# More of layer 1 inside the last attention slot, the last block's first row finished by itself, and the last softmax sums on TensorE

## The chip, the cores and the metric

The kernel runs on one core of a Trainium2 chip. The metric is the time of one execution on the device in microseconds (us). The kernel before was run three times: 3644.64, 3645.58 and 3648.83 us, a median of 3645.58 us. One more execution was recorded by the profiler; it took 3646.8 us, and its first to last instruction span 3645.1 us. All times inside the kernel are from that execution, counted from its first instruction.

## The reference

The input is four images of 64 x 64 pixels with 256 channels, in float32. Two layers are applied in turn.

```python
# layer 0: full self-attention over the 4096 pixels of an image
q = x @ Wq + bq                     # 32 channels
k = x @ Wk + bk                     # 32 channels
v = x @ Wv + bv                     # 256 channels
attn = softmax(einsum('bnd,bmd->bnm', q, k))
x = gamma * einsum('bnm,bmc->bnc', attn, v) + x
# layer 1: perception, two pointwise layers, 3 x 3 local attention
perceived = depthwise_conv3x3(x, w_perc) + b_perc     # 3 outputs per channel: 768
hid = gelu(w_up1 @ perceived + b_up1)                 # 512
h = x + w_up2 @ hid + b_up2                           # 256
q, k, v = split(h @ w_qkv.T + b_qkv)
s[i] = (q * shifted(k, i)).sum(channels) / 16         # i: the 9 neighbours, zero padding
out = h + sum_i softmax(s)[i] * shifted(v, i)
```

The convolution needs the rows above and below a pixel, so a block of rows of layer 1 can be finished only when layer 0 has finished the first row of the next block. The local attention again reaches one row into the next block.

## The kernel before, in words

An image is cut into 8 blocks of 8 rows (512 pixels, `NB`), so there are 32 blocks, numbered 0 to 31 over the four images. The main loop (`for slot in range(NSLOT)`, L695) takes one block of layer 0 per slot. A slot has 16 points. At a point TensorE adds four products of weights and values to the two accumulators of the block (`product`, L279 to L291), at every second point it makes four banks of energies (`energy`, L262), ScalarE takes their exponential (`weight`, L274), and VectorE adds the weights up for the softmax denominator (`add_up`, L293). After the last point `finish` (L305) sums the denominator over the partitions with one product into `dps`, VectorE takes the reciprocal, and scales the two accumulators and adds them to the image held in SBUF (`xp`, seen as `xv`).

Layer 1 follows behind. While slot s runs, VectorE computes the convolution of block s-2 (`perceive`, L337: for each of six output groups one ScalarE operation for the first tap and eight VectorE operations L366, "taps", for the others), TensorE does the pointwise layers of block s-3 (`hidden` L380, four jobs of six products with a Gelu on ScalarE; `update` L405, two jobs into `dx`), then the local attention: `guide` L484 (the rotated queries `g`, copied to `lq`), `scores` L564 (`s`, exponentials `lp`, a mask), `local_values` L533 (`lv`), `border` L505 (`c`, the part of the denominator that comes from the zero padding), `local_sum` L601 (adds the weights up over the pieces into `lsum`), `local_denominator` L629 (one product `ld`, a reciprocal `lrden`) and `local_product` L636 (`lo`, the result). `jobs` (L701) says which of these stands at which point of a slot.

The order on each engine is the order in which the program calls these functions: the kernel is written out by hand, without a scheduler, and every engine takes its instructions in order. An instruction that uses another engine's result, or overwrites what another engine still reads, waits for it; these waits are put in when the program is built, from the tiles that the instructions touch.

PSUM has eight banks: two for the tag `m`, two for `acc`, and the four banks of the one tile `e`. During the slots every job of layer 1 takes a bank from `m`. After the last slot, in the tail, the list `turns` (L774) hands the jobs banks in the order `m, e, acc, m, acc`; a job that gets `e` allocates a new four-bank tile and uses only its first bank (`job_bank`, L98 to L103).

In the last slot (31) VectorE also does three of the six output groups of block 30's convolution, without the block's last row (`extra`, L720 to L724), since that row needs the first row of block 31. After `finish(31)` the tail (L774 to L812) does the rest: the missing rows and groups of block 30, all of the convolution of block 31, the pointwise layers of blocks 29, 30 and 31, and the local attention of blocks 27 to 31. For the last two blocks VectorE does the mask and the sum, for the others GpSimd.

All along, GpSimd adds intermediate results into one tile (`watch`, L158 to L160). At the very end VectorE tests that this tile stayed within bounds (L814 to L823); a register is loaded from the answer, and a slower path (`shifted`) would be taken if it had not.

Of the kernel before, what the change touches and what calls it, by code (L numbers as in the profile page):

```python
# [40 lines left out]
WATCH_MAX = 1.0e25  # L41
# [6 lines left out]
def attention_then_perception_kernel(  # L48
# [34 lines left out]
    def unshifted():  # L83
# [14 lines left out]
        def job_bank(name):  # L98
            turns.append(turns.pop(0))
            if turns[-1] == "e":  # L100
                return psum.tile([P, GRP, NB], F32, tag="e", name=name, bufs=1)[:, 0, :]
            return bank(turns[-1], name)
# [202 lines left out]
        def finish(s):  # L305
            g = s % NBLK
            den = sums.pop(s)

            dps = bank("m", f"dps_{s}")
            nc.tensor.matmul(dps, lhsT=ones, rhs=den[:, 0, :], start=True, stop=True)  # L310
            rden = tile_of([P, NB], "rden", f"rden_{s}", 2)
            nc.vector.reciprocal(rden, dps)  # L312
            os = []
            for c, acc in enumerate(accs.pop(s)):
                o = tile_of([P, NB], "o", f"o_{s}_{c}", 3)
                nc.vector.scalar_tensor_tensor(o, acc, gam[:, 0:1], rden, ALU.mult, ALU.mult)
                os.append(o)
            for c, o in enumerate(os):
                dst = xv[:, c, 1 + g * RB : 1 + (g + 1) * RB, 1 : 1 + W]
                nc.vector.tensor_tensor(  # L320
                    dst, o.rearrange("p (h w) -> p h w", w=W), dst, ALU.add
                )
            watch(den[:, 0, :])
            watch(rden)
            for o in os:
                watch(o)
# [10 lines left out]
        def perceive(s, parts):  # L337
# [5 lines left out]
            def first(i, r0, r1):  # L343
                if i not in percs[s]:
                    if not ahead:
                        perc = tile_of([P, NB], "perc", f"perc_{s}_{i}", NPERC)
                    else:

                        if i % 2 == 0:
                            percs[s, i] = spare(f"perc_{s}_{i}")  # L350
                        perc = percs[s, i - i % 2][:, i % 2, :]
                    percs[s][i] = perc
                tap_of(i, r0, r1, 0)

            def tap_of(i, r0, r1, tap):
# [12 lines left out]
            for n, part in enumerate(parts):  # L368
                if n == 0 or not ahead:
                    first(*part)  # L370
                if ahead and n + 1 < len(parts):
                    first(*parts[n + 1])
                for tap in range(1, TAPS):
                    tap_of(*part, tap)
                    if part[2] - part[1] > 1 or tap % 4 == 0:
                        yield

        whole = [(i, 0, RB) for i in range(NPC)]
# [105 lines left out]
        def guide(s, i):  # L484
# [7 lines left out]
            if s == NSLOT:  # L492
                return
# [11 lines left out]
        def border(s):  # L505
# [19 lines left out]
            pad = tile_of([1, 2 * RB + W], "pad", f"pad_{s}")  # L525
            nc.scalar.activation(pad[:, :n], ps[0:1, :n], AF.Exp, bias=bc, scale=-(C**-0.5))
            nc.gpsimd.tensor_scalar(pad[:, :n], pad[:, :n], 3.0, None, ALU.mult)
            pads[s] = pad

# [3 lines left out]
        def local_values(s, t):  # L533
# [8 lines left out]
            for half in range(2):  # L542
                if s < NSLOT:
                    lvs[s, t, half] = tile_of([P, C], "lv", f"lv_{s}_{t}_{half}", 8)
                else:
# [3 lines left out]
                nc.vector.tensor_tensor(  # L549
                    lvs[s, t, half], ps[:, half * C : (half + 1) * C], blv, ALU.add  # L550
                )
# [12 lines left out]
        def scores(s, half):  # L564
# [4 lines left out]
            tiles, rows = (2, QR) if s < NSLOT else (1, UP)  # L569
            n = tiles * rows * QW  # L570
            for t in range(tiles):
                for kin in range(CH):
# [5 lines left out]
                        rhs=guides[0][:, kin, t * KR : t * KR + rows, columns(half)],  # L578
# [17 lines left out]
            if g == 0:  # L596
                nc.gpsimd.memset(p[P // 2 :, : UP * QW], 0.0)
                if s < NSLOT:
                    nc.gpsimd.memset(p[: P // 2, UP * QW : QR * QW], 0.0)

        def local_sum(s):  # L601
# [12 lines left out]
            pad = pads.pop(s)  # L614
            side = pad[:, : 2 * RB].rearrange("p (w h) -> p h w", w=2)
            edge = one[:, :, 0 : W : W - 1]
            nc.gpsimd.tensor_tensor(edge, edge, side, ALU.add)
            for at, row in ((0, 0), (NBLK - 1, RB - 1)):
                if g == at:
                    above = pad[:, 2 * RB :]  # L620

                    ends = above[:, 0 : W : W - 1]
                    nc.gpsimd.tensor_scalar(ends, ends, 2.0 / 3.0, None, ALU.mult)
                    line = one[:, row, :]
                    nc.gpsimd.tensor_tensor(line, line, above, ALU.add)
# [3 lines left out]
        def local_denominator(s):  # L629
            ps = job_bank(f"ld_{s}")  # L630
            nc.tensor.matmul(ps, lhsT=ones, rhs=lsums.pop(s), start=True, stop=True)  # L631
# [4 lines left out]
        def local_product(s, c):  # L636
# [13 lines left out]
            watch(o)  # L650
# [44 lines left out]
        for slot in range(NSLOT):  # L695
# [24 lines left out]
            extra = iter(())  # L720
            if slot == NSLOT - 1:

                extra = perceive(slot - 1, [(i, 0, RB - 1) for i in range(NPC // 2)])
            for point in range(points):  # L724
# [22 lines left out]
                while stepped < min(n_steps, -(-(point + 1) * n_steps // (points - 2))):  # L747
                    next(conv, None)
                    stepped += 1
                    if stepped % 2:  # L750
                        next(extra, None)
# [17 lines left out]
            for _ in chain(conv, extra):  # L769
                pass  # L770
            finish(slot)


        turns[:] = ["m", "e", "acc", "m", "acc"]  # L774
        conv = chain(
            perceive(
                NSLOT - 2,
                [(i, RB - 1, RB) for i in range(NPC // 2)] + whole[NPC // 2 :],
            ),
            perceive(NSLOT - 1, whole),  # L780
        )
# [7 lines left out]
        last = NSLOT - 1  # L789
        for k in range(NSLOT - LAG_HID, NSLOT):  # L790
            a = k - LAG_ATT + LAG_HID
            if k == last:
                for _ in conv:
                    pass
            run(
                (hidden, k, 0, 6), (hidden, k, 1, 6), (local_denominator, a, 0),
                (hidden, k, 2, 6), (local_product, a, 0, 1), (hidden, k, 3, 6),
# [422 lines left out]
```

## Time and profile before

| | |
|---|---|
| median of three runs | 3645.58 us |
| span of the profiled execution | 3645.1 us |
| TensorE (PE) matmul busy | 3599.6 us, 99% of the span |
| VectorE (DVE) busy | 2448.6 us, 67% |
| ScalarE (ACT) busy | 1176.8 us, 32% |
| GpSimd (POOL) busy | 721.2 us, 20% |
| start of the last `dps` product, that is, the end of slot 31 | 3466.1 us |
| end of the last VectorE operation (L823) | 3638.0 us |

The engines are PE (TensorE matmul), PEld (its weight loads), DVE (VectorE), ACT (ScalarE), POOL (GpSimd) and SP (the queue that issues most transfers). In a line of the profile `L366` is the line of the kernel file, `perc<-xp,wperc,perc` are the tiles written and read, and after the `|` come the busy time, the mean duration of one instruction in ns, and the time that the engine had been idle just before such an instruction, with what ended the idleness. One float32 product of the program appears as two matmul records. A view of waits has lines `engine line waited for: us in total, times, longest us`. A wait for several things is put down to the one that came last.

### The profile page before, as it was taken

The numbers are of one execution on the slowest core, as the hardware profiler recorded it, in microseconds if no ns is written. First come the engines' busy times: TensorE is split into PE (matmuls) and PEld (weight loads), VectorE is DVE, ScalarE is ACT, GpSimd is POOL, SyncE is SP. The second block draws the span as 40 slices with busy tenths as digits, with TensorE's granted clock in tenths as the row PEclk, the third lists the DMA queues.
The fourth block names the chain that finished last, engine by engine and source line by source line (L and its number), as shares of the span: only waits on it lengthen the run. The fifth ranks groups of instructions, "written<-read, shape, count | busy, mean of one in ns | idle before, by whom it ended". The sixth has DMA issues, their size and how long they took to land.

```text
span 3645.1 us, 29412 instructions
## 1 busy us (share of the span) xinstructions
PE 3599.6 (99%) x11350; PEld 1706.7 (47%) x11350; DVE 2448.6 (67%) x2727; ACT 1176.8 (32%) x1324; POOL 721.2 (20%) x725
## 2 busy tenths in 40 slices
PE   9999999999999999999999999999999999999987
PEld 4444444454444444455444444444544444444444
DVE  3385676657666767766677667676666776766884
ACT  2233333323333333332333333333333333333321
POOL 1010112111222221121112222211121122222232
PEclk9999999999999999999999999999999999999999
DMA  3000000010000000101000000011100000000000
GB/s 103 6 3 4 0 9 21 18 44 15 15 15 3 12 15 15 27 23 38 15 15 15 15 3 12 15 27 33 28 15 15 15 15 15 4 12 15 6 10 21
DMA packets 84532, 64.68 MB, mean 18 GB/s; under 512 B 57280, under 2 KB 62528, under 8 KB 84256
## 3 DMA queue, kind: packets, MB, share of 16 engines
q1 hardware_dynamic: 83568, 62.19, 6.3%
q8 instruction: 91, 1.49, 0.2%
q10 hardware_dynamic: 816, 0.53, 0.0%
q14 instruction: 57, 0.47, 0.0%
HBM read 41.52 MB, written 18.81 MB: 17 GB/s over the span
## 4 chain that ended last, share of the span: by engine, by line
PE 97%; DVE 2%; issue 0%; ACT 0%; POOL 0%; DMA 0%; SPq 0%; ACTq 0%; DVEq 0%; POOLq 0%
PE acc L287 49%; PE hid L385 18%; PE e L268 7%; PE dx L411 6%; PE lv L537 3%; PE g L496 3%; PE v L234 3%; PE s L573 2%; PE lo L642 2%; DVE perc L366 1%; PE qk L200 1%; PE ld L631 1%; PE dps L310 1%; DVE lrden L633 0%; DVE rden L312 0%; PE c L520 0%
## 5 line engine op out<-in xcount | busy, mean ns | idle before, releaser
L287 PE MATMUL acc<-p,v 128*128 128x512 f32 x4096 | 1842.2, 595 | 0.1
L366 DVE SCALAR_TENSOR_TENSOR perc<-xp,wperc,perc 128x512 f32<-128x512 f32 (+2 forms) x1560 | 1305.9, 840 | 314.7 <-ACT perc L362 280.7
L287 PEld LDWEIGHTS acc<-p,v 128*128 128x128 f32 x4096 | 769.4, 190 | 917.3 <-issue 913.5
L276 ACT ACTIVATE p<-e 128x1024 f32<-128x1024 f32 x512 | 524.4, 1024 | 1516.1 <-PE e L268 904.1
L385 PE MATMUL hid<-perc,wup 128*128 128x512 f32 x1536 | 689.2, 598 | 1.6 <-DVE perc L366 1.6
L301 DVE TENSOR_TENSOR den<-den,p 128x1024 f32<-128x1024 f32 x480 | 597.0, 1244 | 44.3 <-ACT p L276 40.6
L385 PEld LDWEIGHTS hid<-perc,wup 128*128 128x128 f32 x1536 | 284.2, 190 | 391.4 <-issue 384.3
L268 PE MATMUL e<-qa,ka 32*128 32x512 f32 x2048 | 292.0, 640 | 0.0
L160 POOL TENSOR_TENSOR watched<-watched,lo 128x512 f32<-128x512 f32 x64 | 130.4, 2037 | 624.4 <-DVE lo L649 624.1
L411 PE MATMUL dx<-hid,wup 128*128 128x512 f32 x512 | 232.8, 598 | 0.0
L389 ACT ACTIVATE hid<-hid,bup 128x512 f32<-128x512 f32 x128 | 88.0, 687 | 400.3 <-PE hid L385 400.3
L312 DVE RECIPROCAL rden<-dps 128x512 f32<-128x512 f32 x32 | 107.4, 3358 | 160.4 <-PE dps L310 160.4
L592 POOL TENSOR_TENSOR lp<-lp,near 128x396 f32<-128x396 f32 x60 | 58.1, 970 | 739.0 <-ACT lp L588 739.0
L276 ACT ACT_TABLE_LOAD x116 | 148.8, 1283 | 151.2 <-issue 120.1
L549 DVE TENSOR_TENSOR lv<-lv,blv 128x256 f32<-128x256 f32 x130 | 49.2, 420 | 193.2 <-PE lv L537 193.2
L633 DVE RECIPROCAL lrden<-ld 128x512 f32<-128x512 f32 x32 | 107.4, 3357 | 82.3 <-PE ld L631 82.3
L417 DVE SCALAR_TENSOR_TENSOR h<-dx,bup,xp 128x256 f32<-128x256 f32 x128 | 56.0, 480 | 152.1 <-PE dx L411 149.3
L268 PEld LDWEIGHTS e<-qa,ka 32*128 32x128 f32 x2048 | 79.9, 182 | 164.6 <-issue 162.0
L411 PEld LDWEIGHTS dx<-hid,wup 128*128 128x128 f32 x512 | 94.7, 190 | 129.2 <-issue 120.2
L362 ACT ACTIVATE perc<-xp,bperc,wperc 128x512 f32<-128x512 f32 (+2 forms) x195 | 154.6, 796 | 0.0
L389 ACT ACT_TABLE_LOAD x119 | 152.7, 1283 | 2.2
L537 PE MATMUL lv<-wlv,h 128*128 128x256 f32 x520 | 128.6, 390 | 12.3 <-DVE h L417 11.0
(91 smaller groups left out, 2030.9 us busy)
## 6 DMA issues: line engine op xcount, KB each, us to landing
xp<-in_x SPq DMA_DIRECT2D x30, 528.0 KB, 4.1
out<-lo SPq DMA_DIRECT2D x60, 256.0 KB, 2.0
xc<-in_x SPq DMA_DIRECT2D x48, 256.0 KB, 3.8
qa<-packed SPq DMA_DIRECT2D x124, 64.0 KB, 2.1
ka<-st SPq DMA_DIRECT2D x124, 16.0 KB, 1.8
packed<-st SPq DMA_DIRECT2D x31, 64.0 KB, 1.9
wup<-in_w_up SPq DMA_DIRECT2D x1, 1536.0 KB, 7.0
xp<-in_x SPq DMA_DIRECT2D x4, 264.0 KB, 3.9
```

What stands on the lines that cost most here:

```text
L160: nc.gpsimd.tensor_tensor(watched, watched, values, ALU.add)
L234: nc.tensor.matmul(ps[:, i * C : (i + 1) * C], lhsT=xc[:, kin, bass.ts(2 * pair + i, P)], rhs=wv[:, kin, :], start=(kin == 0), stop=(kin = ...
L268: nc.tensor.matmul(e[:, j, :], lhsT=key[rows, :], rhs=queries[s][rows, :], start=True, stop=True,)
L276: nc.scalar.activation(p, energies[s, G][:, 2 * half : 2 * half + 2, :], AF.Exp)
L287: nc.tensor.matmul(accs[s][c], lhsT=v[:, 2 * half + i, bass.ts(c, P)], rhs=p[:, i, :], start=(first and i == 0), stop=(G == NG - 1 and hal ...
L301: nc.vector.tensor_tensor(den, den, p, ALU.add)
L362: nc.scalar.activation(acc, win, AF.Identity, bias=bperc[:, half, j : j + 1], scale=wt)
L366: nc.vector.scalar_tensor_tensor(acc, win, wt, acc, ALU.mult, ALU.add)
L385: nc.tensor.matmul(ps, lhsT=wup1[:, i, bass.ts(d, P)], rhs=percs[s][i], start=(i == 0), stop=(i == NPC - 1),)
L389: nc.scalar.activation(hids[s][:, d, :], ps, AF.Gelu, bias=bup1[:, d : d + 1])
L411: nc.tensor.matmul(ps, lhsT=wup2[:, d, bass.ts(c, P)], rhs=hids[s][:, d, :], start=(d == 0), stop=(d == NHC - 1),)
L537: nc.tensor.matmul(ps[:, half * C : (half + 1) * C], lhsT=keys_of(s, t, half, kin), rhs=wlv[:, kin, :], start=(kin == 0), stop=(kin == CH ...
```

## The change

There are six edits. Nothing before slot 31 is touched: on every engine the list of instructions is the same up to a point inside slot 31.

1. In slot 31 the list `jobs` is replaced. The jobs of block 28 stand closer together, and the points after them take in the four `hidden` jobs, both `update` jobs and both `local_values` jobs of block 29, with `local_sum`, `local_denominator` and `local_product` of block 27 and `border` of block 28. `guide` and `scores` of block 29 stay in the tail.
2. VectorE's list for slot 31 becomes the whole convolution of block 29 and then, for all six groups of block 30, the taps that need no row of block 31, and the others without the last row (`upper`). It was three groups of block 30, one step for every two of block 29.
3. `finish` becomes a generator, and for block 31 it works in two parts: row 0, and later rows 1 to 7. Between the two stand the 18 taps of block 30's last row (`lower`), and on TensorE the `guide` jobs of block 29.
4. In the tail `spread` is allocated once, as a four-bank tile, and the jobs are given slices of it in the order `spread[0], spread[1], m, spread[2], spread[3], m`.
5. The last block's `local_sum` is dropped. `local_denominator(31)` instead makes eight products of `ones` with the pieces of the weights, and with the border weights laid into a zeroed tile.
6. The watching changes: for the last blocks GpSimd adds the squares of the local values (twelve operations of 128 x 256) and the weights instead of the last sum and the last results; the test at the end sums the tile first (one reduction and two operations on 128 x 1), with the bound 1e22 for 1e25.

```diff
         def job_bank(name):
             turns.append(turns.pop(0))
-            if turns[-1] == "e":
-                return psum.tile([P, GRP, NB], F32, tag="e", name=name, bufs=1)[:, 0, :]
-            return bank(turns[-1], name)
+            return bank("m", name) if turns[-1] == "m" else turns[-1]
...
-        def finish(s):
+        def finish(s, parts=((0, RB),)):
...
+            for r0, r1 in parts:
+                n = slice(r0 * W, r1 * W)
+                nc.vector.reciprocal(rden[:, n], dps[:, n])
+                for c, o in enumerate(os):
+                    nc.vector.scalar_tensor_tensor(
+                        o[:, n], acc[c][:, n], gam[:, 0:1], rden[:, n], ALU.mult, ALU.mult
+                    )
...
+                if r1 == RB:
+                    watch(den[:, 0, :])
+                    watch(rden)
+                    for o in os:
+                        watch(o)
+                yield
...
+        LOW = TAPS - 3
+        upper = [
+            part for i in range(NPC)
+            for part in ((i, range(LOW), 0, RB), (i, range(LOW, TAPS), 0, RB - 1))
+        ]
+        lower = [(i, range(LOW, TAPS), RB - 1, RB) for i in range(NPC)]
...
+                if s >= NSLOT - 1:
+
+                    square = tile_of([P, 2, NB], "den", f"lv_{s}_{t}_{half}_2")[:, 0, :C]
+                    nc.gpsimd.tensor_tensor(square, lv, lv, ALU.mult)
+                    nc.gpsimd.tensor_tensor(watched[:, :C], watched[:, :C], square, ALU.add)
...
         def local_denominator(s):
             ps = job_bank(f"ld_{s}")
-            nc.tensor.matmul(ps, lhsT=ones, rhs=lsums.pop(s), start=True, stop=True)
+            if s < NSLOT - 1:
+                nc.tensor.matmul(ps, lhsT=ones, rhs=lsums.pop(s), start=True, stop=True)
+            else:
+
+                pv = ps.rearrange("p (h w) -> p h w", w=W)
+                side, line = both(pads["last"])
+                todo = [
+                    (pv[:, rows, columns(half)], near_ws[block, half][:, t, of, :])
+                    for half in range(2) for (block, t), rows, of in pieces(s)
+                ]
+                todo += [(pv[:, :, 0 : W : W - 1], side), (pv[:, RB - 1, :], line)]
+                for i, (to, p) in enumerate(todo):
+                    nc.tensor.matmul(
+                        to, lhsT=ones, rhs=p, start=(i == 0), stop=(i == len(todo) - 1),
+                        skip_group_check=True,
+                    )
...
-            extra = iter(())
             if slot == NSLOT - 1:
 
-                extra = perceive(slot - 1, [(i, 0, RB - 1) for i in range(NPC // 2)])
+
+                jobs = [
+                    job(hidden, k, 0), job(hidden, k, 1) + job(local_denominator, a),
+                    job(hidden, k, 2), job(local_product, a, 0) + job(hidden, k, 3),
+                    job(local_product, a, 1) + job(update, k, 0),
+                    job(update, k, 1) + job(local_values, k, 0),
+                    job(guide, k, 0) + job(local_values, k, 1), job(guide, k, 1),
+                    job(scores, k, 0) + job(hidden, k + 1, 0),
+                    job(scores, k, 1) + job(local_sum, k - 1) + job(hidden, k + 1, 1),
+                    job(hidden, k + 1, 2) + job(local_denominator, a + 1),
+                    job(hidden, k + 1, 3), job(update, k + 1, 0) + job(border, k),
+                    job(local_product, a + 1, 0) + job(update, k + 1, 1),
+                    job(local_product, a + 1, 1) + job(local_values, k + 1, 0),
+                    job(local_values, k + 1, 1),
+                ]
+                conv = chain(conv, perceive(slot - 1, upper))
+                n_steps += NPC * (TAPS - 1 + 3)
...
-        turns[:] = ["m", "e", "acc", "m", "acc"]
...
+        spread = psum.tile([P, GRP, NB], F32, tag="e", name="spread", bufs=1)
+        turns[:] = [spread[:, 0], spread[:, 1], "m", spread[:, 2], spread[:, 3], "m"]
+        last = NSLOT - 1
+        conv = perceive(last, whole)
...
+        finishing = finish(last, ((0, 1), (1, RB)))
+        next(finishing)
+        run((guide, last - 2, 0, 0), (guide, last - 2, 1, 0))
+        for _ in perceive(last - 1, lower):
+            pass
+        next(finishing)
         run(
...
+            (scores, last - 2, 0, 1), (scores, last - 2, 1, 1), (local_sum, last - 3, 0),
+            (hidden, last - 1, 0, 6), (hidden, last - 1, 1, 6), (local_denominator, last - 3, 0),
+            (hidden, last - 1, 2, 6), (local_product, last - 3, 0, 1), (hidden, last - 1, 3, 6),
+            (local_product, last - 3, 1, 1), (border, last - 2, 0), (update, last - 1, 0, 4),
+            (update, last - 1, 1, 4), (local_values, last - 1, 0, 2), (guide, last - 1, 0, 2),
+            (local_values, last - 1, 1, 2), (guide, last - 1, 1, 2), (scores, last - 1, 0, 2),
+            (scores, last - 1, 1, 2), (local_sum, last - 2, 0),
+        )
+        for _ in conv:
+            pass
...
-        test = [tile_of([P, NB], "o", f"test_{i}", 3) for i in range(2)]
...
+        good = tile_of([P, 3], "good", "good")
+        nc.vector.tensor_reduce(good[:, 0:1], watched, axis=AX.X, op=ALU.add)
```

A number after the function and its block in `run` is how many taps of block 31's convolution VectorE does after that job.

## The prediction

> **What bounds the kernel now.** I read the page's top first, then the busy times by stage, then the waits of PE, then single rows for durations.
>
> The slices of the page show PE full until the last two:
>
> ```profile
> PE   9999999999999999999999999999999999999987
> DVE  3385676657666767766677667676666776766884
> ```
>
> So only the end can be won. The stages from the start of slot 31 (3361) to the last VectorE operation (3638), columns as in the heading:
>
> ```profile
> core 0: us, PE busy (x) PEld busy (x) DVE busy (x) ACT busy (x) POOL busy (x), PEclk, DMA share, GB/s
> 3361.00:3466.00 105.00, 105.00 (x323) 49.26 (x323) 88.79 (x105) 38.13 (x43) 24.48 (x21) 1.00 0.02 5
> 3466.00:3500.00 34.00, 32.58 (x93) 15.86 (x91) 31.59 (x46) 7.96 (x14) 9.40 (x6) 1.00 0.00 0
> 3500.00:3571.00 71.00, 59.09 (x196) 33.37 (x196) 60.34 (x80) 16.20 (x24) 25.98 (x26) 0.93 0.04 15
> 3571.00:3600.00 29.00, 28.69 (x86) 14.82 (x87) 6.60 (x8) 3.46 (x6) 8.73 (x9) 1.00 0.05 19
> 3600.00:3638.00 38.00, 23.08 (x126) 17.79 (x124) 24.53 (x39) 5.32 (x11) 13.77 (x16) 0.92 0.08 28
> ```
>
> Slot 31 is bound by PE (105 of 105, VectorE 89). From 3466 to 3571 VectorE bounds (92 of 105) and PE idles 13.3; then PE again; at the end a chain through all engines. PE is idle for 277 - 248.4 = 28.6 us, all in the tail. Who ends these waits, from 3360 on:
>
> ```profile
> PE lv L537 <- DVE h L417: 11.0, 3, 6.6
> PE good_sum L822 <- DVE good L820: 6.5, 1, 6.5
> PE ld L631 <- POOL lsum L625: 5.1, 1, 5.1
> PE hid L385 <- DVE perc L366: 1.6, 1, 1.6
> PE ld L631 <- POOL lsum L617: 1.2, 1, 1.2
> PE lv L537 <- ACT h L398: 1.1, 1, 1.1
> PE s L573 <- ACT lq L500: 0.9, 2, 0.4
> PE s L573 <- ACT lq L491: 0.9, 1, 0.9
> ```
>
> The 11.0 is VectorE being behind with the convolution; 5.1 and 6.5 are the end chain. A long wait costs more than itself. In the timeline of PE:
>
> ```profile
> 3624.98 2.07 PE L631 MATMUL ld<-lsum,ones 128*128 128x512 f32 x2 [5.08 <-POOL lsum L625]
> 3626.85 3.93 PE L642 MATMUL lo<-lp,lv 128*128 128x99 f32 x24
> ```
>
> The same pair takes 1.02 and the same 24 records 3.26 elsewhere. With two slow `lv` groups after the 6.6 wait (1.19 for 0.59, 2.93 for 1.45) the two long waits cost 3.8 us on top: 32.4 us to be won at most.
>
> **What the skill says.** (1) PSUM — Partial Sum Buffer, "PSUM bank collisions raise a hardware error": accesses of two engines must be kept apart by bank (and quadrant). That would leave the four banks of `spread` independent. The waits of the built program are wider, see below; which cost that has, the trace of before cannot show, since there each job allocates its tile. (2) TensorE: Matmul & The Clock Gate, "What's actually happening": half clock after an idle window of about 3.4 us. The trace agrees for 5.1 and 6.6 us of idleness and shows no slowing after 1.6. (3) GPSIMD Engine Reference, "1. Specifications": GpSimd shares SBUF interfaces with VectorE's two-input operations. The trace agrees: a tap is 0.75 us alone and 1.76 beside a `watch`.
>
> **The change part by part.** PE's work stays the same but for eight products in place of one for `ld`(31): 872 columns for 512, +0.6 us. Work moved into slot 31: four `hidden` jobs 20.6 (24 records take 10.3), two `dx` 6.9, two `lv` 3.4, two `lo` 3.1, `ld` 0.9, `c` 0.3, together 35.2 us; slot 31 grows by that and the tail shrinks by it. A gain is possible only by fewer waits, so I list the waits of PE after the change, all of them, and set them against the 32.4. The issues that move past SP are results of block 27; they queue behind nothing that PE needs.
>
> *Slot 31.* `lv`(28) now stands right after `dx`(28,1), and waits for `h`. PE reaches the end of that `dx` at about 3413.8 (before it started at 3418.1; two groups of `acc`, 6.9, and one of `e`, 1.1, now stand later). VectorE's list to that `h`: from 3361.2, `finish` 7.1, first copy 1.75, five sums at 1.22, `lrden` 3.36, two `lo` 1.4, `h` 0.9, 41 taps (it was about two thirds of that) at 0.79 = 32.4, and 4 for GpSimd's `watch` beside them: 57, so 3418.2. PE waits 4.3. Bounds: 0 if VectorE keeps up, 7. The later points have VectorE ahead again (taps of block 29 done about 10 us before `hidden`(29) needs them).
>
> *The tile `spread`.* In the built program a product into any bank of `spread` waits for the last reader of any other bank of it, because it is one tile. The row of jobs is two in `spread`, one in `m`; so every second job of a pair starts only when the first has been read out. Each such pair costs PE the reader's time plus some 0.2 for the hops: Gelu 0.69, `lq` 0.69, `lp` 0.50, two `lv` 0.76, two `h` 0.87, `lo` 0.68. By the list of the tail: `g`(29) 0.9, `lo`(28) 0.9, `dx`(30) 0.7 and 1.2, `lv`(30) 0.9, `s`(30) 0.8 and 0.7, `ld`(29) 0.9, `hidden`(31,3) 0.95, `g`(31) 1.05, `lv`(32) 0.9, `s`(31) 0.6, `s`(32) 0.4: 10.9. `dx`(31) waits for the border of block 30 with its table load (1.28 in the trace): 1.8. `s`(31,1) waits for `lp`(31,0), and this stands in ScalarE's queue behind the border of block 31, whose tile GpSimd zeroes only after its twelve squares: 2.6. Together 15.3.
>
> Two of them are longer. `hidden`(30,0) waits for `lp`(29,1). On ScalarE that stands behind the first taps of block 31, which need the second part of `finish`. From the end of `dps`: part one 1.3, 18 taps of 64 at 0.32 = 5.8, reciprocal of 448 2.95, two `o` 1.4, first `xp` 1.2, two first taps 1.5, `lp` 0.5, hops 0.2: 14.9. PE has `g` and `s` to do, 6.1 and 1.5 of waits: 7.6. So PE waits 7.3, and row 0 finished early brings nothing: the perceptions are complete after 7.1. `hidden`(30,2) waits for `lrden`(28), 3.36 and hops: 3.6. Both 10.9. After the first the clock is low: 1.8 (the mean of the two seen). For waits under 5 I take no slow clock; if it came at all four of over 3 us, 5 more.
>
> *The end.* `ld`(30) waits for its sum: exponential, masks, `lsum` on VectorE (0.48 and six at 0.33), and GpSimd's border addition behind two `watch` of `lp`: 3.6. Then `lo`(30,1) waits for `lrden`(30) since both are in `spread`: 2.3; `ld`(31) for `lo`(30,1) to be read: 1.9; `lo`(31,1) for `lrden`(31): 2.3; `good_sum` for the last results and the reduction: 2.8. Together 12.9, where before it was 5.1 + 1.2 + 6.5 = 12.8 and the low clock. The edits that shorten this chain (no `lsum`(31), no `watch` of the last `lo`, a test of 0.7 for 1.8) are eaten by these.
>
> *Small ones:* `s` on `lq` 0.6, `lv` on `h` 0.3 twice: 1.2. A first product after a wait takes 0.70 for 0.59 (trace, 3571.2); 14 more waits: 1.4. Not in the durations: turns between kinds of product on PE, beside which a part of the waits will lie; I take 2.5 off.
>
> Sum: 4.3 + 15.3 + 10.9 + 12.9 + 1.2 + 1.8 + 1.4 + 0.6 - 2.5 = 45.9 against 32.4: **+13.5 us**. On the profiled span 3658.6; on the median of the three runs (3645.58, half a us above the span) 3659.
>
> **Rivals.** (a) *The waits by tile cost nothing, the four banks work as four.* Place: PE's pairs in the tail. Then the 15.3 and 10.9 go, but PE meets VectorE and GpSimd: `ld`(28) waits 4.4 for GpSimd (four `watch`, two masks, the sum, about 11 us from 3514), `lv`(30) 7.0 for `h`, `ld`(30) 6.5, `good_sum` 7.4, with 4.3 in the slot and 1.2 small: 30.8, and twice the low clock: **3646**, no change. It decides where the pairs and the two long waits come to under 14 us. For it: the hardware needs only banks apart. Against it: the waits are instructions of the program. A gain beyond 0.2% would need VectorE's 4.3 and 7.0 to fall away too (**3634**); it has 48 taps of block 31 in the way. (b) *VectorE bounds slot 31.* 96 taps at 0.84 (the page's mean) are 81, sums 20, the rest 20, that is 121 of the 140 us; by the first points alone it is behind, and `watch` stretches taps. If its 4 us of stretch become 8, and `hidden`(29) waits too: **3665**. (c) *GpSimd's twelve squares at the end.* At half of a `watch` of 128 x 512 (1.27 alone) they take 0.65 each; beside VectorE up to 1.0 (the mask of 128 x 396 took 0.96 to 1.32). Then `pad`, `lp` and `ld`(30) come 4 later: **3663**. (d) *The low clock after each wait over 3 us*: **3664**.
>
> **How the numbers follow.** Forecast, with (c) or (d) in part, 3653 to 3667: 0.70. (a), or half of it: 0.15, with 0.04 beyond it for a gain. (b), or (c) and (d) together, over 3667: 0.11. A measurement tells about 0.2% from no change, 7.3 us, so: under 3638.3 0.04, to 3652.9 0.15, above 0.81. Range: 3649 (the upper half of (a) left out) to 3668.
>
> **What would show it.** Right: the end of slot 31 at about 3505 (3466 + 35 + 4); a wait of 4 of `lv` for `h` in it; a wait of about 7 of the first `hid` of the tail for ScalarE's `lp`, of 3.6 for `lrden`, and some fifteen of about 0.9 for readers of `spread`; waits of PE of 40 to 48 us from 3360 on; the tail shorter by only some 25. Wrong: PE waits under 32 us, or the first `hid` of the tail right after the small taps.

## The result: 13 us slower, and the profile after

The changed kernel takes 3660.58 us (median of six runs, 3656.27 to 3663.83) against 3647.8 for the kernel before (six runs beside it). The ratio is 1.0036, with a 95% interval of 1.0024 to 1.0049. The forecast was 3659 us, with a range of 3649 to 3668.

The rows of PE and VectorE in the page's 40 slices, which showed the end before:

```profile
PE   9999999999999999999999999999999999999987
DVE  3385676657766766766677667666666676677873
```

PE's row is the same as before: at this scale its loss still shows only in the last two slices. The busy times by stage, for slot 31 (to `dps` of block 31), the tail up to 3600, and the end:

```profile
core 0: us, PE busy (x) PEld busy (x) DVE busy (x) ACT busy (x) POOL busy (x), PEclk, DMA share, GB/s
3361.00:3505.96 144.96, 141.98 (x437) 68.96 (x437) 119.64 (x140) 53.21 (x60) 33.10 (x27) 0.99 0.02 8
3505.96:3600.00 94.04, 78.29 (x233) 39.86 (x232) 66.82 (x91) 19.14 (x28) 32.27 (x32) 0.96 0.02 9
3600.00:3654.00 54.00, 37.68 (x168) 26.22 (x166) 23.57 (x37) 5.88 (x13) 22.60 (x30) 0.91 0.07 25
sum 293.00, PE 257.95 PEld 135.04 DVE 210.03 ACT 78.23 POOL 87.97; mean PE 85.98 PEld 45.01 DVE 70.01 ACT 26.08 POOL 29.32
```

The stretch from the start of slot 31 to the last VectorE operation has grown from 277 to 293 us. PE's idle time in it went from 28.6 to 35.05 us (293.00 - 257.95), and its busy time from 248.44 to 257.95 with the same products but for `ld`(31), whose eight products take 2.2 us where one takes 1.0. So 6.5 us are more waiting, 1.2 are `ld`(31), and some 8 are products that run longer. The waits of PE from 3360 on (engine, tile and line, releaser, total, times, longest; the largest rows):

```profile
PE spread L396 <- ACT lp L610: 5.2, 1, 5.2
PE spread L396 <- DVE lrden L675: 3.5, 1, 3.5
PE spread L684 <- DVE lrden L675: 3.3, 2, 1.9
PE spread L659 <- POOL lsum L647: 3.2, 1, 3.2
PE lv L554 <- DVE h L428: 3.0, 1, 3.0
PE spread L595 <- ACT lp L610: 2.9, 2, 2.3
PE good_sum L882 <- DVE good L878: 2.6, 1, 2.6
PE spread L422 <- ACT pad L540: 1.7, 1, 1.7
PE spread L554 <- ACT lq L509: 1.6, 2, 0.8
PE spread L422 <- DVE h L428: 1.0, 1, 1.0
```

Of these only the waits for `lsum`, `h` at L554 and `good` are for data that the product reads. The others are for the reader of another bank of `spread`: a `hid` product reads neither `lp` nor `lrden`. Longer products stand behind waits of both kinds. The timeline of PE (start, us, line, tiles, records, idle before and releaser):

```profile
3416.82 2.93 PE L554 MATMUL lv<-wlv,h 128*128 128x256 f32 x6 [2.98 <-DVE h L428]
3520.13 8.06 PE L396 MATMUL spread<-perc,wup 128*128 128x512 f32 x12 [5.22 <-ACT lp L610]
3528.03 5.31 PE L396 MATMUL hid<-perc,wup 128*128 128x512 f32 x12
3537.65 5.42 PE L396 MATMUL spread<-perc,wup 128*128 128x512 f32 x12 [3.45 <-DVE lrden L675]
```

Six such records of `lv` take 1.56 us at 3554.7 in the kernel before. The 12 records of a `hid` job take 8.06 us behind the wait of 5.22 and 5.31 in the next job; behind the wait of 3.45 they take 5.42.

### The profile page after: what moved, and what is told of

Its sections match the earlier page's. It is cut to its first block, busy times and chain, and to the rows that moved or that the text cites. A ratio compares the mean times of both kernels' runs of the same rounds, so it can differ in the third digit from the quotient of the medians.

```text
span 3660.1 us, 29450 instructions
## 1 busy us (share of the span) xinstructions
PE 3609.1 (99%) x11364; PEld 1710.7 (47%) x11364; DVE 2446.3 (67%) x2719; ACT 1183.9 (32%) x1326; POOL 727.2 (20%) x737
## 4 chain that ended last, share of the span: by engine, by line
PE 96%; DVE 3%; ACT 0%; issue 0%; DMA 0%; POOL 0%; SPq 0%; ACTq 0%; DVEq 0%; POOLq 0%
PE acc L286 48%; PE hid L396 17%; PE e L267 7%; PE dx L422 6%; PE v L233 3%; PE lv L554 3%; PE g L505 3%; PE lo L684 2%; PE s L595 2%; DVE perc L369 1%; PE qk L199 1%; PE dps L310 1%; PE spread L396 1%; PE ld L659 1%; DVE rden L315 0%; DVE lrden L675 0%
## 5 line engine op out<-in xcount | busy, mean ns | idle before, releaser
L369 DVE SCALAR_TENSOR_TENSOR perc<-xp,wperc,perc 128x512 f32<-128x512 f32 (+1 forms) x1554 | 1303.8, 840 | 313.5 <-ACT perc L365 278.4
L396 PE MATMUL hid<-perc,wup 128*128 128x512 f32 x1476 | 662.6, 598 | 0.0
L396 PEld LDWEIGHTS hid<-perc,wup 128*128 128x128 f32 x1476 | 273.1, 190 | 375.5 <-issue 370.7
L422 PE MATMUL dx<-hid,wup 128*128 128x512 f32 x488 | 222.4, 598 | 0.0
L315 DVE RECIPROCAL rden<-dps 128x512 f32<-128x512 f32 (+2 forms) x33 | 107.6, 3260 | 159.2 <-PE dps L310 159.2
L365 ACT ACTIVATE perc<-xp,bperc,wperc 128x512 f32<-128x512 f32 x192 | 153.9, 803 | 9.2 <-PE hid L396 5.2
L675 DVE RECIPROCAL lrden<-ld 128x512 f32<-128x512 f32 x28 | 94.0, 3357 | 75.1 <-PE ld L659 75.1
L159 POOL TENSOR_TENSOR watched<-watched,lrden 128x512 f32<-128x512 f32 x32 | 63.0, 1969 | 334.1 <-DVE lrden L675 334.1
```

The costliest lines, as they stand in the source:

```text
L159: nc.gpsimd.tensor_tensor(watched, watched, values, ALU.add)
L365: nc.scalar.activation(acc, win, AF.Identity, bias=bperc[:, half, j : j + 1], scale=wt)
L369: nc.vector.scalar_tensor_tensor(acc, win, wt, acc, ALU.mult, ALU.add)
L396: nc.tensor.matmul(ps, lhsT=wup1[:, i, bass.ts(d, P)], rhs=percs[s][i], start=(i == 0), stop=(i == NPC - 1),)
L422: nc.tensor.matmul(ps, lhsT=wup2[:, d, bass.ts(c, P)], rhs=hids[s][:, d, :], start=(d == 0), stop=(d == NHC - 1),)
```

## The experiments

Executions of these kernels differ by some 3 us before slot 31 begins, though the code up to there is the same: `dps` of block 30 starts between 3356.69 and 3357.38 in five of the 13 profiled executions and between 3359.77 and 3360.14 in the other eight. So beside the medians stand the lengths in the trace: slot 31 from `dps`(30) to `dps`(31), and the tail from `dps`(31) to the write of `bad`, the last VectorE operation.

| kernel | median us | ratio to before, 95% interval | slot 31 | tail | sum |
|---|---|---|---|---|---|
| before | 3645.58 to 3647.80 | 1 | 105.97 | 171.73 | 277.70 |
| changed | 3660.58 | 1.0036 [1.0024, 1.0049] | 145.99 | 147.85 | 293.84 |
| e1 changed, four tiles | 3645.07 | 0.9995 [0.9986, 1.0003] | 147.64 | 130.87 | 278.51 |
| e8 changed, old turns | 3644.04 | 0.9994 [0.9985, 1.0002] | 146.29 | 130.76 | 277.05 |
| e3 before, one tile `spread` | 3665.22 | 1.0052 [1.0039, 1.0066] | 105.97 | 191.86 | 297.83 |
| e12 before, four tiles | 3648.15 | 1.0002 [0.9994, 1.0011] | 105.97 | 173.42 | 279.39 |
| e4 changed, `lv`(28) later | 3654.07 | 1.0025 [1.0016, 1.0035] | 141.36 | 146.41 | 287.77 |
| e2 changed, `lp`(29) first | 3665.31 | 1.0046 [1.0033, 1.0060] | 146.28 | 154.12 | 300.40 |
| e5 changed, `pad` early | 3661.28 | 1.0041 [1.0025, 1.0056] | 145.98 | 147.52 | 293.50 |
| e10 changed, no split | 3666.01 | 1.0057 [1.0042, 1.0073] | 146.09 | 148.10 | 294.19 |
| e6 = e1 + e4 + e5 | 3638.48 | 0.9980 [0.9972, 0.9988] | 141.35 | 129.10 | 270.45 |
| e11 = e8 + e4 + e5 | 3639.07 | 0.9978 [0.9969, 0.9987] | 141.35 | 128.68 | 270.03 |
| e9 = e6 + filler | 3640.73 | 0.9980 [0.9972, 0.9988] | 141.35 | 129.61 | 270.96 |

### The shared tile: e1, e8, e3 and e12

e1 keeps the change, its order of jobs and its turns. The tile of four banks that holds the energies is given a pool of its own; this pool is closed after slot 31, and its banks are opened again under four tags, one [P, NB] tile for each tag:

```diff
-        spread = psum.tile([P, GRP, NB], F32, tag="e", name="spread", bufs=1)
-        turns[:] = [spread[:, 0], spread[:, 1], "m", spread[:, 2], spread[:, 3], "m"]
+        ectx.close()
+        epool[0] = fctx.enter_context(tc.tile_pool(name="four", bufs=1, space=PSUM))
+        turns[:] = ["x0", "x1", "m", "x2", "x3", "m"]
...
```

> The changed kernel with four tiles of one bank each in the place of the one four-bank tile spread; order of jobs and banks as before, only the whole-tile waits go. Theory (the whole-tile waits are what makes the change slower): the waits of PE for readers of another bank, some 23 us of the 35 from 3360 on, and 5 to 7 us of slowed products after them go; PE then meets VectorE and GpSimd (ld of block 28 for its sum, lv of block 30 for h, the end chain), which gives back about 15. Time 3646, between 3642 and 3650, that is 10 to 18 below the changed kernel and level with the kernel before. Rival (the waits only show work that is late anyway, VectorE and GpSimd set the end): 3657 to 3661, the waits of PE change their names and keep their sum of 35.

Measured: 3645.07 us. All the waits of PE from 3360 on in e1:

```profile
PE ld L663 <- POOL lsum L651: 10.8, 2, 5.5
PE lv L558 <- DVE h L432: 6.0, 2, 3.0
PE good_sum L887 <- DVE good L883: 5.8, 1, 5.8
PE s L599 <- ACT lq L513: 0.9, 2, 0.4
```

Every row that waited for the reader of another bank is gone; what remains is waiting for data, 23.5 us for the 34.5 of the changed kernel. That the rival, a mere change of names with the sum kept, is false is seen in both the sum and the time. The waits for data are longer than in the changed kernel (10.8 for 3.2 at `ld`), as forecast: PE now meets GpSimd and VectorE. VectorE has next to no pause from `dps`(31) to its last tap:

```profile
3508.70:3574.30 65.60, 56.26 (x172) 30.30 (x170) 63.47 (x89) 16.52 (x24) 28.23 (x28) 0.92 0.02 8
```

63.47 of 65.60 us. This, and no longer the banks, now bounds the first part of the tail. From `dps`(30) to `bad` PE is idle for 23.9 us in e1 and 35.0 in the changed kernel, and busy for 254.8 and 259.0: of the 15.3 us between the two, 11.1 are waits and 4.2 are products that run longer.

e8 takes the banks back to what the kernel before had, with a tile for each job:

```diff
-        turns[:] = [spread[:, 0], spread[:, 1], "m", spread[:, 2], spread[:, 3], "m"]
+        turns[:] = ["m", "e", "acc", "m", "acc"]
...
```

> The changed kernel with the turns of the kernel before in its tail: m, e, acc, m, acc, each job with a tile of its own. This undoes the edit of the banks alone. Theory (the whole-tile waits cost some 15): s(29,0) and hidden(30,0) now wait for finish to read acc, about 6 us, and the others of the waits go: 3645 to 3652. Rival (the loss is in the rest of the change): 3658 to 3662.

Measured: 3644.04 us, just better than expected. The wait that was foreseen is there, and is the largest:

```profile
PE s L597 <- DVE o L319: 6.7, 1, 6.7
```

So five separate banks are as good as six. e8 also says what the rest of the change is worth: 277.05 against 277.70 us in the trace, a ratio of 0.9994 whose interval holds 1. The whole loss is in the one edit.

e3 and e12 do that edit in the kernel before. e3 has one tile:

```diff
-        turns[:] = ["m", "e", "acc", "m", "acc"]
+        spread = psum.tile([P, GRP, NB], F32, tag="e", name="spread", bufs=1)
+        turns[:] = [spread[:, 0], spread[:, 1], "m", spread[:, 2], spread[:, 3], "m"]
...
```

e12 has four, made as in e1:

```diff
-        turns[:] = ["m", "e", "acc", "m", "acc"]
+        ectx.close()
+        epool[0] = fctx.enter_context(tc.tile_pool(name="four", bufs=1, space=PSUM))
+        turns[:] = ["x0", "x1", "m", "x2", "x3", "m"]
...
```

> The kernel before with one edit of the change alone: in its tail the jobs go to the four banks of one tile spread and to m in turn, in place of m, e, acc, m, acc. Theory: every second job of a pair waits for the reader of the first, 0.7 to 0.9 us each and more at lrden and at the exponentials; part of it lies in the stretch up to 3571 where PE idles 13 us for VectorE anyway. 8 to 15 us more: 3655 to 3662. Rival (the hardware's banks are independent, and the old turns of five had waits of their own): within 2 us of 3647.

> The kernel before with four separate tiles in its tail, the turns x0, x1, m, x2, x3, m. Against it stands the kernel before with the same turns over one tile, at 3665. Theory (the price of the shared tile is its waits, not the turns): 3644 to 3648, so that one tile or four makes 17 to 21 us in this kernel; no gain over the kernel before, because its long waits are for VectorE. Rival (the new turns are themselves worse than the old): 3652 to 3660.

Measured: 3665.22 and 3648.15 us. e12 ends 0.15 above its range, e3 3 us above. The expectation of e3 priced waits alone, and these were in its range: from `dps`(30) to `bad` PE's idle time grew by 10.4 us over the kernel before (39.0 for 28.6), since the new waits took the place of most of the 11 us in which `lv` waited for `h`. PE's busy time grew by another 9.7 (259.0 for 249.3) with the same products. The largest waits of e3 behind the shared tile:

```profile
PE spread L409 <- DVE lo L647: 4.3, 1, 4.3
PE spread L640 <- DVE lo L647: 4.0, 1, 4.0
PE spread L629 <- DVE lo L647: 3.5, 1, 3.5
PE spread L383 <- DVE lrden L631: 3.4, 1, 3.4
```

A pair costs more than the 0.7 to 0.9 of one read-out where the reader, here the product with `lrden` on VectorE, stands behind other work in its engine's queue: the 4.0 us are a wait for a `lo` behind six taps of 5.35 us in sum. With the same turns over four tiles these waits are gone. In both kernels the shared tile costs 15 to 17 us (3660.58 - 3645.07, 3665.22 - 3648.15), slower products included.

### Slot 31: e4

e4 moves the two `local_values` jobs of block 28 one point later:

```diff
-                    job(update, k, 1) + job(local_values, k, 0),
-                    job(guide, k, 0) + job(local_values, k, 1), job(guide, k, 1),
+                    job(update, k, 1),
+                    job(guide, k, 0) + job(local_values, k, 0),
+                    job(guide, k, 1) + job(local_values, k, 1),
```

> The changed kernel with the two local_values jobs of block 28 one point later in slot 31, so that an e group and an acc group stand between dx(28,1) and lv(28,0). Theory: the wait of 3.0 of lv for h and the slowed six products (2.93 for 1.45) go, and nothing takes their place: PE is busy in all of slot 31 and the end of slot 31 comes 3.5 to 4.5 us earlier: 3655 to 3657. Rival (VectorE bounds slot 31): the last weights or the small taps are not earlier, the gain shows again as a longer wait at hidden(30,0), time within 1 us of 3660.

Measured: 3654.07 us, 1 us below the range. In the trace slot 31 is shorter by 4.63 us, just over the 3.5 to 4.5 expected. The tail, which the edit doesn't touch, is shorter by 1.4: there `dx`(31,0) took 3.70 us for 5.40 and `s`(31,1) 1.61 for 2.93 behind the same waits as in the changed kernel. The medians are 6.5 apart, but six of the ten runs lie between 3652.49 and 3655.05 and four between 3661.02 and 3661.38; what parts them is open. What the edit is worth is read from the length of slot 31. The timeline of PE in e4, at the place where `lv` waited:

```profile
3407.19 3.60 PE L422 MATMUL dx<-hid,wup 128*128 128x512 f32 x8
3410.63 3.60 PE L286 MATMUL acc<-p,v 128*128 128x512 f32 x8
3414.15 1.14 PE L267 MATMUL e<-qa,ka 32*128 32x512 f32 x8
3415.22 1.98 PE L505 MATMUL g<-h,wg 128*128 128x512 f32 x4
3417.05 1.89 PE L554 MATMUL lv<-wlv,h 128*128 128x256 f32 x8
```

No idle time and no slow record; in all of slot 31 PE is busy for 141.36 of 141.36 us. VectorE does not bound slot 31.

### Waits that were not on the path: e2, and the split: e10

e2 puts the two score jobs of block 29 ahead of the first step of block 31's convolution:

```diff
-            (scores, last - 2, 0, 1), (scores, last - 2, 1, 1), (local_sum, last - 3, 0),
+            (scores, last - 2, 0, 0), (scores, last - 2, 1, 2), (local_sum, last - 3, 0),
```

> The changed kernel with the two score jobs of block 29 ahead of the first step of block 31's convolution, so that ScalarE's exponential of (29,1) stands ahead of its two first taps, which wait for the last part of finish. Theory: the wait of 5.2 of the first hidden product for that exponential goes and with it the slowed 12 products (8.06 for 5.31); hidden(30,0) starts at about 3515 and runs 5.3. Up to 8 us less; since lrden(28) and the sum of block 28 on GpSimd then come into view, 4 to 8 less: 3653 to 3657. Rival (hidden(30,0) is early but everything behind it waits for VectorE, which gets no earlier): the wait moves to lrden or h, and the time stays within 2 us of 3660.

Measured: 3665.31 us. The theory of this experiment fell. The wait of 5.2 did go, as PE's timeline in e2 shows, but the time came back in the next two rows:

```profile
3512.77 5.42 PE L396 MATMUL spread<-perc,wup 128*128 128x512 f32 x12 [0.59 <-ACT lp L610]
3526.80 2.07 PE L659 MATMUL spread<-lsum,ones 128*128 128x512 f32 x2 [3.47 <-POOL lsum L647]
3534.80 8.20 PE L396 MATMUL spread<-perc,wup 128*128 128x512 f32 x12 [5.92 <-DVE lrden L675]
```

`hidden`(30,2) waits for `lrden`(28), since both are in the one tile, and VectorE comes to `lrden`(28) only behind its convolution. VectorE's timeline in the changed kernel:

```profile
3519.67 14.54 DVE L369 SCALAR_TENSOR_TENSOR perc<-xp,wperc,perc 128x512 f32<-128x512 f32 x14
3534.24 3.36 DVE L675 RECIPROCAL lrden<-spread 128x512 f32<-128x512 f32 x1
```

and in e2:

```profile
3516.95 14.53 DVE L369 SCALAR_TENSOR_TENSOR perc<-xp,wperc,perc 128x512 f32<-128x512 f32 x14
3531.39 3.35 DVE L675 RECIPROCAL lrden<-spread 128x512 f32<-128x512 f32 x1
```

Counted from `dps`(31), `lrden` starts at 28.3 and 28.2 us, and `hidden`(30,2) at 31.7 and 31.6. The early `hidden`(30,0) only lengthened the wait for `lrden` from 3.45 to 5.92, as the rival had it, and the 12 records of `hidden`(30,2) now ran slow on the path (8.20 for 5.42). At the end e2 lost more: from 3626 on most of its products ran slow, for instance

```profile
3639.02 3.35 PE L684 MATMUL spread<-lp,lv 128*128 128x99 f32 x12 [0.47 <-DVE lrden L675]
```

where the changed kernel took 1.80. That end has the same instructions in both, and the trace does not show why they ran slower; one of the five runs took 3659.52 us.

e10 undoes the splitting of the last `finish`:

```diff
-        finishing = finish(last, ((0, 1), (1, RB)))
+        finishing = finish(last)
```

> The changed kernel without the splitting of the last finish: all 512 columns at once, then the lower row of the convolution of block 30. Theory (row 0 finished by itself brings nothing, since the first hidden product waits for an exponential that stands behind the whole of finish on ScalarE): within 2 us of 3660; the first hidden product starts 1 us later or earlier at most. Rival (the split keeps the perceptions of block 30 off the path): 4 to 6 us more, 3664 to 3666.

Measured: 3666.01 us, 5 us above the changed kernel and just above the rival's range. The first `hid` comes 2.85 us earlier from `dps`(31) than with the split, not within 1: `xp` is complete sooner, and so are the first taps on ScalarE before `lp`. But `hidden`(30,2) again starts 31.3 us after `dps`(31), and behind the longer wait it runs slow:

```profile
3537.53 8.05 PE L396 MATMUL spread<-perc,wup 128*128 128x512 f32 x12 [6.89 <-DVE lrden L675]
```

The changed kernel took 5.42. So e10 is 2.3 us behind at the first `hid` of block 31 (70.4 us after `dps`(31), 68.1 with the split). The tail still ends level, 148.10 for 147.85, because `dx`(31,0) and `s`(31,1) took 3.70 and 1.61 us here and 5.40 and 2.93 in the changed kernel, behind the same waits. The profiled execution (3662.53 us) is also the fastest of the four. The intervals of the two ratios overlap. Whether the split is worth anything in the changed kernel is therefore not shown; the runs lean to the rival.

### The end chain: e5, and the combined kernels

e5 zeroes the tile of the last border on GpSimd ahead of the squares:

```diff
-                pads["last"] = tile_of([P, NB], "st", f"pad_{s}")
-                nc.gpsimd.memset(pads["last"], 0.0)
...
+        def zero_pad(s):
+            pads["last"] = tile_of([P, NB], "st", f"pad_{s}")
+            nc.gpsimd.memset(pads["last"], 0.0)
...
-            (update, last, 1, 0), (below, NSLOT, 0), (local_values, last, 0, 0),
+            (update, last, 1, 0), (below, NSLOT, 0), (zero_pad, last, 0), (local_values, last, 0, 0),
```

> The changed kernel with the tile of the last border zeroed on GpSimd ahead of the twelve squares instead of behind them. Theory (the squares hold up the end chain): ScalarE's exponential of the border no longer waits for GpSimd, the wait of 2.3 of s(31,1) for lp(31,0) falls to about 0.6, its slowed eight products (2.93) to 1.6, and ld of block 30 comes 2 to 3 us earlier: 3656 to 3658. Rival (the two additions of the weights to watched, or VectorE's masks and sums, hold ld of block 30 back as long): its wait grows from 3.2 to 5 or 6 and the time stays at 3659 to 3661.

Measured: 3661.28 us. The wait of `s`(31,1) fell from 2.31 to 0.59 and its eight products from 2.93 to 1.61 us, and `ld`(30) starts 2.9 us earlier after `dps`(31). Yet the tail is only 0.33 shorter. The timeline of PE in e5:

```profile
3632.14 2.07 PE L661 MATMUL spread<-lsum,ones 128*128 128x512 f32 x2 [3.33 <-POOL lsum L649]
3634.01 3.19 PE L686 MATMUL lo<-lp,lv 128*128 128x99 f32 x12
3637.66 3.35 PE L686 MATMUL spread<-lp,lv 128*128 128x99 f32 x12 [0.47 <-DVE lrden L677]
3647.46 2.65 PE L686 MATMUL spread<-lp,lv 128*128 128x99 f32 x12 [1.86 <-DVE lrden L677]
```

The three groups of `lo` took 2.23, 1.80 and 1.80 in the changed kernel. Slower products gave the gain back: neither the theory nor the rival, which looked to GpSimd and VectorE, had this.

e6 puts the edits of e1, e4 and e5 together.

> The four separate tiles, the two local_values jobs of block 28 one point later, and the border's tile zeroed ahead of the squares, together. Theory (the three waits are separate and add up): from the 3645 of the four tiles 4 us for slot 31 and 2 for the end chain: 3639, between 3636 and 3642. Since VectorE works without a pause for 65 us from dps(31) on with four tiles, only what makes slot 31 end earlier and what comes after VectorE's last tap can count; both edits are of that kind. Rival (VectorE is behind already in slot 31, so that its list ends no earlier): 3643 to 3646.

Measured: 3638.48 us, 22 us under the changed kernel and 0.2% faster than the kernel before (ratio 0.9980, an interval without 1). Against e1, slot 31 is shorter by 6.3 and the tail by 1.8 us. Of the 6.3, 1.7 is one group of `acc` that ran 5.32 us behind `lv` in e1 and 3.67 in the changed kernel.

e11 has the edit of e8 in the place of that of e1.

> The changed kernel with the turns m, e, acc, m, acc of the kernel before, the two local_values jobs of block 28 one point later, and the border's tile zeroed ahead of the squares: the combined kernel with five separate banks in place of six. Theory (once no tile is shared the number of banks doesn't matter, since VectorE sets the tail from dps(31) to its last tap): 3636 to 3640, level with the combined kernel's 3638.5. Rival (the wait of s(29,0) for finish to read acc, 6.7 us, puts PE behind VectorE): 3641 to 3645.

Measured: 3639.07 us. Five separate banks do as well as six here too.

e9 fills PE's gap before `ld`(30) in e6 with products that nobody reads:

```diff
-            (scores, NSLOT, 1, 0), (local_denominator, last - 1, 0),
+            (scores, NSLOT, 1, 0), (filler, 8, 0), (local_denominator, last - 1, 0),
```

> The combined kernel with eight more products of 128x396 (a sum that nobody reads) between the scores of block 32 and ld of block 30, where PE waits 4.3 us for the sum. Theory (the wait itself slows the products behind it): with the gap filled to some 1.5 us, ld of block 30 takes 1.0 in place of 2.07 and the 24 records of lo 3.3 in place of 5.16; the end chain is then VectorE's and only ld stands on it: 1 us less, 3636.5 to 3638. Rival (the slow products there have another cause, such as the change of the kind of product): ld stays at 2.07, lo at 4 to 5, time 3638 to 3640.

```profile
3609.37 5.51 PE L854 MATMUL filler<-near,ones 128*128 128x396 f32 x16
3614.71 1.02 PE L665 MATMUL ld<-lsum,ones 128*128 128x512 f32 x2
3615.57 3.26 PE L690 MATMUL lo<-lp,lv 128*128 128x99 f32 x24
```

Measured: 3640.73 us, above both ranges, with the same ratio as e6. The mechanism holds: behind busy time `ld` takes 1.02 for 2.07 and `lo` 3.26 for 5.16. The time doesn't improve. Eight products are 16 records and took 5.51 us, twice what I had reckoned, so that `ld` came 0.9 later after the scores; and the end is VectorE's, for `good_sum` now waits 6.5 us in place of 4.6.

## Why the prediction was right, step by step

The forecast was +13.5 us; the medians are 12.8 apart and the profiled spans 15.0. The cause is as forecast, the tile `spread`. But the forecast put the whole loss into idle time of PE (44.6 - 2.5 against 28.6, +13.5) and held slower and extra products level (1.8 + 1.4 + 0.6 against 3.8). Measured were 6.5 us more idle time and 9.5 more busy time. That the sum came out so near is partly luck.

- *Work moved into slot 31*, 35.2 us: without its wait (e4) slot 31 is 35.4 us longer than before. Right. The tail was to be shorter by 25 and is by 23.9.
- *`lv`(28) waits for `h`*, 4.3: the wait is 2.98, and the slow products behind it add 1.4; taking both away gave 4.63. The size is right, the make-up isn't: a third of it is the low clock, which this step had left out.
- *The pairs in `spread`*, 15.3: the rows of this kind come to 12.5. The mechanism is shown by e1, e3 and e12. Each is a little shorter than reckoned.
- *The two long waits*, 7.3 and 3.6: measured 5.2 and 3.5. As waits right, as costs the step failed: e2 took the first away and gained nothing. They are one stretch whose end VectorE sets, 28 us after `dps`(31), with `lrden`(28) behind 14 taps. The step should have followed VectorE's queue to `lrden` instead of adding up PE's waits. Its remark that row 0 finished early brings nothing stays open after e10.
- *The end chain*, 12.9: measured 9.9; the largest part of the difference is `ld`(31), which waited 0.78 and not 1.9. The 2.6 for GpSimd's squares, counted with the pairs, was measured at 2.3. e5 took that wait away, and neither its trace nor its median got better: slower `lo` groups gave the gain back.
- *The low clock*, 1.8: this is the term that was badly mis-sized. The groups from slot 31 on that took longer than the same group elsewhere come to 9.2 us: `hid` 2.75, `dx`(31,0) 1.70 (5.40 for 3.70), `lv` 1.4, `s`(31,1) 1.3, `ld` 1.1, `lo` 0.5, `s`(32) 0.4. Rival (d), slowing after every wait over 3 us at 5 us more, was too mild and had the wrong places. The waits were over-sized by 10 us in sum (44.6 for 34.5) and this under-sized by 7: two errors of opposite sign. Against the kernel before, the low clock is 5.4 of the 9.5 us by which PE's busy time grew (9.2 - 3.8). The eight products of `ld`(31), reckoned at 0.6, are 1.2; the other 2.9 are not itemised, first products after the waits among them, for which the forecast had 1.4. The mark "waits of PE of 40 to 48 us" was missed accordingly.
- *Rival (a)*, 3646 if the banks worked as four: this is e1, at 3645.07. It was wrong as a forecast of the change and right as one of the repair, with its reason: PE then waits for VectorE and GpSimd. Its waits were over-sized too, 30.8 for the 23.5 of e1. The Trainium skill (PSUM — Partial Sum Buffer, "PSUM bank collisions raise a hardware error") names the bank, within a group of partitions, as what two engines must not access at the same time. e1 agrees, since with separate tiles a product and a read-out in different banks run side by side: ScalarE's Gelu reads `hid`(30,0) from 3523.1 to 3523.8 us while PE, busy from 3515.3 to 3525.8, writes `hid`(30,1). The waits in the changed kernel belong to the tile.
- *Rivals (b) and (c)*: e4 and e5 speak against them; slot 31 ran without a wait of PE once `lv` was moved, and freeing the end chain of the squares shortened the changed kernel's tail by 0.3 us only.

On the low clock, the trace of before already held a warning against "For waits under 5 I take no slow clock":

```profile
3509.27 2.93 PE L537 MATMUL lv<-wlv,h 128*128 128x256 f32 x6 [2.84 <-DVE h L417]
```

The prediction put this group down to the 6.6 us wait that had ended 4 us earlier. In the changed kernel six such records of block 28 take the same 2.93 us behind a wait of 2.98, with no long wait ahead of them.

## What to carry to other kernels

A tile of several banks is one thing to the program's waits, even if each job writes its own bank: give each job a tile of its own, and check the waits for readers that have nothing to do with the product. Before a wait is priced, follow the queue of the engine that ends the next one; in the tail of the changed kernel a wait of 5 us was free, because VectorE's 14 taps ended later anyway. And reckon the slow products behind a wait together with the wait.

## What was not expected of the hardware

Products ran slow after shorter waits than I had reckoned with: after 1.70 us (`dx`(31,0), 5.40 for 3.70), 2.31 (`s`(31,1), 2.93 for 1.61) and 2.98 us (`lv`), and not after 3.45 (5.42 for 5.31) in the same execution. The same wait at the same place has different effects in different executions. `dx`(31,0) in the changed kernel and in e2:

```profile
3602.93 5.40 PE L422 MATMUL spread<-hid,wup 128*128 128x512 f32 x8 [1.70 <-ACT pad L540]
3602.85 3.70 PE L422 MATMUL spread<-hid,wup 128*128 128x512 f32 x8 [1.69 <-ACT pad L540]
```

e5 has it slow too, e4 and e10 don't. The Trainium skill (TensorE: Matmul & The Clock Gate, "What's actually happening") gives an idle window of about 3.4 us, which it calls free-running. Slow products after waits of 1.70 to 2.98 us do not fit one idle window of that length, and the length of one wait doesn't decide it here. Nor does the clock always come back: in e2 the share granted from 3625 to 3657 was 0.57, though PE was busy 23.5 of those 32 us, against 0.87 for the same 84 records in the changed kernel:

```profile
3625.00:3657.00 32.00, 23.49 (x84) 21.17 (x84) 18.16 (x24) 1.70 (x5) 11.68 (x15) 0.57 0.08 31
3627.00:3654.00 27.00, 16.08 (x84) 14.13 (x84) 18.59 (x25) 1.71 (x5) 11.37 (x14) 0.87 0.10 39
```

Why one execution recovers and another does not, these runs do not settle.
